# Step 2's VectorE work in two stages on two row blocks in turn: a two-layer graph kernel on one Trainium2 core

## The chip, the cores and the metric

The kernel runs on one core of one Trainium2 chip. The metric is the device time of one execution in microseconds. The engines are named as in the profile: PE (matrix products; PEld its weight loads), DVE (VectorE), ACT (ScalarE), POOL (GpSimd), SP (SyncE, which here only issues DMAs). Each engine works through its own instructions in order.

## The reference, cut to what matters

With N = 2708 nodes and 256 features, layer 0 computes `x = layernorm(x + relu([x, adj @ x] @ weight + bias))`. Layer 1 is this, followed by one more `layernorm(x + ...)`:

```
R = (adj + I) / rowsum                # sparse: about 8 entries a row
for n in range(2):
    logits = (Xa W1' W2') (Xa W3')'
    probs  = softmax(logits)
    keep   = the largest probs of a row, until their sum reaches 0.9
    A      = probs * keep / sum(probs * keep)
    Xf = R @ Xf
    Xa = A @ Xa
    Z += Xf @ U1[n]' + Xa @ U2[n]'
out = layernorm(X + Z) * g + b
```

Everything is float32. What is hard is `keep`: the smallest kept value of each row has to be found exactly, without sorting 2708 values, and equal values at the limit have to be taken in order of their place.

## The kernel before

Rows are worked on in NB = 22 blocks of P = 128 (the last, EDGE, has 20 rows). The program's stages follow each other in time: layer 0 with the dense adjacency (0 to about 285 us); step 1 of layer 1 (to 755 us), in whose begin `u1_project` makes x1 @ U1 and stores it; and step 2 (from 755 us on), the loop over `per` at L1127, which the change is about. Everything is written in the order in which each engine is to issue it; no scheduler moves anything. Waits between engines, and between instructions of one engine that depend on each other, are semaphores that the framework sets.

**Step 2, one period per row block.** In period `per` three blocks are in work. Block per+2: `logits` (PE) and `exps2` (ACT) write its exponentials, 128 x 2708, into one of four buffers es[0..3], chosen by `e2(t)`; `begin_search` (DVE) begins the search for the row's limit. Block per+1: `try_act` (ACT) evaluates two guesses of the limit with passes over the row (Relu and Sign with a summed output). Block per: DVE alone. `last_level` forms from the guesses a level that lies surely above the limit; `finish2` then

1. sets everything at or above the level to zero and sums what is below, in one pass over 2720 columns (L975, e to w),
2. takes the 8 largest of each of 20 segments of 136 columns (L978), 160 candidates,
3. sorts out the 48 largest by six rounds of MAX8 and MATCH_REPLACE8 (`put_in_order`, L575 and L577),
4. finds the limit th from their running sums (L988 to L993), and how many of the values equal to th are to be kept in each of WS = 5 parts of the row (L997 to L1003),
5. marks those in place (MATCH_REPLACE8 over 544 columns, five times, L1006), and
6. masks e in one pass (L1009) and takes the reciprocal of the kept sum (L1011).

Block per-1: PE turns the masked e (`turn`, transposes, L525), ACT copies them to wT (L528), PE multiplies with ya (`products`, L562). The period is written in NG = 6 slots g; `finish2` is a generator whose `yield`s place its parts in the slots.

**The R products.** Beside that, `r_units` (L729) issues 16 pieces of R @ Xf in each of periods 0 to 9 and 11 to 21. R is sparse: for each row block, POOL gathers 7 x 128 rows of the operand from DRAM by indirect DMA (`y_load`, L697) into one of two slots of yg, and the block's own rows come as an eighth group. The first pass (s = 0) takes x1 U1[1] from DRAM (yf_d), own rows by SP (L714); `r_out` adds to it, in place, the SBUF tile v that holds x1 U1[0] (L752), and stores the sum in v_d (L754). The second pass (s = 1, from period 11) gathers from v_d and takes its own rows from v; `r_out` calls `arrive`. When a block has both its R part and its attention part (`arrive`, L767; what came first waits in za_d and is fetched by `za_load`), `final_slot` normalizes it: statistics on DVE (L1036), scaling on ACT (L1046), two tensor operations on POOL (L1061, L1062), and the store.

**Buffers.** Tile pools hand out slots by tag in turn. "V" (22.5 KB a partition) holds layer 0's y0 and then v; "x1" holds x1 and then tile1, cut into w (DVE's work area) and scr (ACT's thrown-away output); the tag "in" has three slots for bases.

The functions that the diff touches, and their callers:

Of the kernel before, what the change touches and what calls it, by code (L numbers as in the profile page):

```python
# [9 lines left out]
FP = mybir.dt.float32  # L10
# [18 lines left out]
WS = 5  # L29
# [119 lines left out]
def fast_path(ctx, tc, c, flags, fint, xT_d, x_d, w0_d, b0_d, w1_d, w2_d, w3_d, u1_d, u2_d, g_d, b_d):  # L149
# [492 lines left out]
    v = big.tile([P, NB, D], FP, tag="V", name="v")  # L642

    def u1_project(t):
        p = rows(t)
        pz = ps_acc()
        for j in range(DC):
            nc.tensor.matmul(pz[:p], lhsT=x1T[:, j, t * P:t * P + p],  # L648
                             rhs=c.u1[:, j].rearrange("p s e -> p (s e)"), start=j == 0, stop=j == DC - 1)
        nc.scalar.copy(v[:p, t, :], pz[:p, :D])  # L650
        yf = work.tile([P, D], FP, tag="h", name="yf", bufs=5)
        nc.scalar.copy(yf[:p], pz[:p, D:])
        nc.sync.dma_start(out=c.yf_d[:p, t, :], in_=yf[:p])
# [53 lines left out]
    def r_load(s, m):  # L707
        if m not in a_in:
            a_load(m)
        if (s, m) not in y_in:  # L710
            y_load(s, m)
        y = y_in.pop((s, m))
        if s == 0:
            nc.sync.dma_start(out=y[:rows(m), CC, :], in_=c.yf_d[:rows(m), m, :])  # L714
        r_in[s, m] = a_in.pop(m), y

    def r_units(n):
        for _ in range(n):
            s, m = r_queue[0]
            p = rows(m)  # L720
            if not r_now:
                r_now[:] = [ps_misc(), 0]
                if m + 1 < NB:
                    r_load(s, m + 1)
            acc, k = r_now
            a, y = r_in[s, m]
            kw = CW if k < CC else p
            rhs = v[:p, m, :] if s and k == CC else y[:kw, k, :]
            nc.tensor.matmul(acc[:p, :D], lhsT=a[:kw, k, :p], rhs=rhs, start=k == 0, stop=k == CC)  # L729
            r_now[1] += 1  # L730
            if k == CC:
                r_now.clear()
                r_queue.pop(0)
                r_in.pop((s, m))
                base = za_load(m) if s else None
                later[1].append(lambda s=s, m=m, acc=acc, base=base: r_out(s, m, acc, base))

# [11 lines left out]
    def r_out(s, m, acc, base):  # L749
        p = rows(m)  # L750
        if s == 0:
            nc.vector.scalar_tensor_tensor(v[:p, m, :], acc[:p, :D], rinv[:p, m:m + 1], v[:p, m, :],  # L752
                                           op0=ALU.mult, op1=ALU.add)
            nc.sync.dma_start(out=c.v_d[:p, m, :], in_=v[:p, m, :])  # L754
            if m == NB - 1:
                r_load(1, 0)
        else:
            arrive(m, base, acc, rinv[:p, m:m + 1])
# [21 lines left out]

    def e2(t):
        return es[(t + 2) % 4]
# [16 lines left out]
    class Block:  # L799
# [3 lines left out]
        def __init__(self, t):  # L803
            self.t, self.p = t, rows(t)
            self.all = small.tile([P, 20], FP, tag="st2", name="st2", bufs=4)
            names = "z0 z1 z2 rz nz roots half relu sign n kept m d g l0 l1 l2 u0 u1 few".split()
            for i, n in enumerate(names):
                setattr(self, n, self.all[:self.p, i:i + 1])
            self.l, self.u = (self.l0, self.l1), (self.u0, self.u1)
            self.z = bulk[:self.p, 0, t:t + 1]  # L810
            self.nmax = small.tile([P, 1], FP, tag="nmax", name="nmax", bufs=3)[:self.p]
# [11 lines left out]
    def begin_search(b):  # L823

        nc.vector.tensor_reduce(b.z, b.all[:b.p, :NL], AX.X, ALU.add)
        nc.vector.reciprocal(b.rz, b.z)
        nc.vector.tensor_scalar(b.nz, b.z, -1.0, None, op0=ALU.mult)
        nc.vector.tensor_scalar(b.l0, b.roots, b.roots, b.rz, op0=ALU.mult, op1=ALU.mult)

# [83 lines left out]
    w = tile1[:, :NW]  # L913
    scr = tile1[:, NW:]
# [40 lines left out]
    def last_level(b):  # L955


        nc.vector.scalar_tensor_tensor(b.n, b.relu, b.rz, b.few, op0=ALU.mult, op1=ALU.is_lt)
        nc.vector.scalar_tensor_tensor(b.g, b.l1, TOP_S, b.u1, op0=ALU.mult, op1=ALU.is_gt)
        nc.vector.tensor_scalar(b.kept, b.l2, b.n, 1.0e-20, op0=ALU.mult, op1=ALU.max)  # L960
        nc.vector.scalar_tensor_tensor(b.kept, b.g, b.l1, b.kept, op0=ALU.mult, op1=ALU.max)
        level(b, b.kept)
# [3 lines left out]
    def finish2(b):  # L966

        t, p = b.t, b.p
        sc = small.tile([P, 3 + 2 * WS], FP, tag="sc", name="sc", bufs=3)
        num, run = bulk[:p, 5:, t], sc[:p, :WS]  # L970
        need, below, mass, tot = (bulk[:p, i, t:t + 1] for i in range(1, 5))
        nk = sc[:p, WS:WS + 1]
        th = b.m
        e = e2(t)[:p]
        nc.vector.scalar_tensor_tensor(w[:p], e, b.d, e, op0=ALU.is_lt, op1=ALU.mult, accum_out=below)  # L975
        cand = small.tile([P, NS2 * 8], FP, tag="cand", name="cand", bufs=2)
        for i in range(NS2):
            nc.vector.max(cand[:p, 8 * i:8 * i + 8], w[:p, SEG2 * i:SEG2 * (i + 1)])  # L978
            if i in (2, NS2 // 2 + 1):
                yield  # L980
        yield
        srt = small.tile([P, TOP1 + 1], FP, tag="srt", name="srt", bufs=3)
        s = srt[:p, :TOP2]
        put_in_order(srt, TOP2, cand, p)
        yield
# [3 lines left out]
        nc.vector.tensor_tensor_scan(x[:p, 1:TOP2 + 1], s, s, 0.0, op0=ALU.add, op1=ALU.bypass)  # L989
        nc.vector.scalar_tensor_tensor(q_, x[:p, 1:TOP2 + 1], need, s, op0=ALU.is_ge, op1=ALU.mult)  # L990
        nc.vector.tensor_reduce(th, q_, AX.X, ALU.max)
        nc.vector.scalar_tensor_tensor(q_, x[:p, :TOP2], need, s, op0=ALU.is_lt, op1=ALU.mult, accum_out=mass)
        nc.vector.tensor_scalar(q_, q_, th, None, op0=ALU.is_equal, op1=ALU.add, accum_out=nk)  # L993

        eq = small.tile([P, NS2 * 8], FP, tag="spare", name="eq", bufs=1)
        part = small.tile([P, WS, 8], FP, tag="part", name="part", bufs=1)
        nc.vector.tensor_scalar(eq[:p], cand[:p], th, None, op0=ALU.is_equal)  # L997
        nc.vector.tensor_reduce(num, eq[:p].rearrange("p (s k) -> p s k", s=WS), AX.X, ALU.add)
        nc.vector.tensor_tensor_scan(run, num, num, 0.0, op0=ALU.add, op1=ALU.bypass)
        nc.vector.scalar_tensor_tensor(run, num, nk, run, op0=ALU.add, op1=ALU.subtract)  # L1000
        nc.vector.tensor_tensor(part[:p], run[:, :, None].to_broadcast([p, WS, 8]),
                                ranks[:p, None, :].to_broadcast([p, WS, 8]), op=ALU.is_gt)
        nc.vector.tensor_scalar(part[:p], part[:p], th, None, op0=ALU.mult)  # L1003
        W = NW // WS
        for i in range(WS):
            nc.vector.match_replace(w[:p, W * i:W * (i + 1)], part[:p, i, :], e[:, W * i:W * (i + 1)], 3.0e38)  # L1006
            if i == WS // 2:
                yield
        nc.vector.scalar_tensor_tensor(e, w[:p], th, e, op0=ALU.is_gt, op1=ALU.mult, accum_out=tot)  # L1009
        ra = small.tile([P, 1], FP, tag="ra", name="ra")  # L1010
        nc.vector.reciprocal(ra[:p], tot)  # L1011
        ras[t] = ra
# [102 lines left out]
    for b in (b0, b1, b2):  # L1115
        exps2(b, 2, *logits(1, b.t, 2))
        r_units(3)
        if b is b2:
            try_dve(b0, 1)
        begin_search(b)  # L1120
        if b is b0:
            try_dve(b0, 0)
# [4 lines left out]
    for per in range(NB + 1):  # L1127
        if per == NB:
# [3 lines left out]
        b_dve = blocks.get(per)  # L1132
        t_mul = per - 1 if per else None
        if per:
            accs[t_mul] = ps_acc(t_mul)
        masks = None
        b_exp = None
        if per and per + 2 < NB:
            b_exp = blocks[per + 2] = Block(per + 2)
        for g in range(NG):  # L1140
# [11 lines left out]
            elif per:  # L1152
# [9 lines left out]
            if t_mul != EDGE:  # L1162
                products(1 if per else 0)
            if b_exp and g in (0, 1, 3):
                exps2(b_exp, (g + 1) // 2, *lg)
            if b_act:
                for k, part in {0: ((0, 0),), 1: ((0, 1), (0, 2), (0, 3)), 2: ((1, 0),), 3: ((1, 1), (1, 2), (1, 3))}.get(g, ()):
                    try_act(b_act, k, part)
            if g == 0:
                if b_dve:  # L1170
                    last_level(b_dve)
                    masks = finish2(b_dve)
                    next(masks)
                final_slot(0)
                if per > 1:

# [3 lines left out]
            elif masks:  # L1180
                next(masks, None)
                if b_exp and g == 5:
                    begin_search(b_exp)
            for f in now:
                f()
            if g and (per < NB or g < NG - 1):
# [17 lines left out]
    nc.vector.tensor_reduce(flags[:, 5 * NB:6 * NB], bulk[:, 5:, :].rearrange("p w t -> p t w"), AX.X, ALU.max)  # L1204
    nc.vector.tensor_scalar(flags[:, 5 * NB:6 * NB], flags[:, 5 * NB:6 * NB], 8.0, None, op0=ALU.is_ge)
# [389 lines left out]
```

## Time and profile before

| | us |
|---|---|
| median of 3 runs | 1348.48 (1345.78 to 1349.26) |
| the profiled execution, its own time | 1345.32 |
| its span | 1343.5 |
| first long pass of step 2 (L975) begins | 766.3 |
| last mask of step 2 (L1009) ends | 1322.6 |
| busy in the span: PE / DVE / ACT / POOL | 1246.7 / 1045.5 / 753.4 / 640.1 |
| mean granted PE clock | 0.971 |

A span runs from the first instruction to the last; the time of an execution holds some two microseconds more. A row of a timeline has the start in us from the span's begin, the duration, the engine, the line in the kernel, the operation, what it writes and reads, and in brackets the idle time before it and what ended that. The ends of PE's matmuls are modelled, and consecutive ones overlap: how fast PE goes is read from start to start.

### The profile page before, as it was taken

How to read it: one execution, taken by the hardware profiler on the slowest of the kernel's cores; microseconds unless marked ns; L12 is line 12 of the kernel's file. 1: busy time of each engine (PE TensorE's matmuls, PEld its weight loads, DVE VectorE, ACT ScalarE, POOL GpSimd, SP SyncE). 2: the span in 40 equal slices, each digit the busy share in tenths (PEclk: the TensorE clock that was granted, in tenths of full speed). 3: DMA queues.
4: the chain of work that ended last, by engine and by line, in shares of the span. 5: the costliest groups of instructions: out<-in, count | busy, mean ns of one | idle time of the engine just before them, and what ended most of it. 6: DMA issues, size and time to landing. Idle time of an engine off the chain costs nothing.

```text
span 1343.5 us, 18721 instructions
## 1 busy us (share of the span) xinstructions
PE 1246.7 (93%) x5676; PEld 881.0 (66%) x5676; DVE 1045.5 (78%) x3488; ACT 753.4 (56%) x1366; POOL 640.1 (48%) x591
## 2 busy tenths in 40 slices
PE   8999999989899999999999789999998998999885
PEld 6877878833467666667666367676765765666663
DVE  2544545865998888777751599999999999999997
ACT  1010001035556556655555567887878888999851
POOL 1000000004465522777654478877725757777770
PEclk9999999989899999999999889999998999999988
DMA  7455554512131210232223355554522633454341
GB/s 188 163 172 162 164 164 143 166 51 72 60 98 57 71 58 9 74 102 81 71 68 97 98 166 169 148 160 147 161 66 92 191 119 122 150 172 146 122 144 37
DMA packets 92829, 157.92 MB, mean 118 GB/s; under 512 B 16356, under 2 KB 65196, under 8 KB 92720
## 3 DMA queue, kind: packets, MB, share of 16 engines
q1 hardware_dynamic: 66434, 100.59, 23.6%
q0 software_dynamic: 20544, 51.17, 13.4%
q10 hardware_dynamic: 5742, 4.89, 1.3%
q8 instruction: 47, 0.77, 0.2%
q14 instruction: 62, 0.51, 0.1%
HBM read 125.33 MB, written 31.26 MB: 117 GB/s over the span
## 4 chain that ended last, share of the span: by engine, by line
PE 54%; DVE 38%; ACT 4%; issue 2%; POOL 1%; DMA 1%; SPq 0%; ACTq 0%; DVEq 0%; POOLq 0%
PE acc L562 16%; PE acc L255 15%; PE lg L505 6%; DVE cand L978 6%; DVE w L1006 5%; DVE e L1009 5%; DVE w L975 4%; PE tr L525 4%; DVE srt L575 3%; DVE spare L577 3%; PE misc L676 3%; PE acc L648 2%; PE acc L460 2%; PE misc L424 2%; PE misc L390 2%
## 5 line engine op out<-in xcount | busy, mean ns | idle before, releaser
L528 ACT COPY wT<-tr 128x512 f32<-128x512 f32 (+2 forms) x258 | 131.9, 519 | 223.4 <-PE tr L525 219.0
L562 PE MATMUL acc<-ya,wT 128*128 128x256 f32 (+1 forms) x924 | 236.3, 396 | 12.1 <-ACT wT L528 11.7
L697 POOL DMA_INDIRECT yg<-yf_d,ix x154 | 194.8, 1265 | 78.7 <-PE misc L729 40.6
L697 POOL DMA_INDIRECT yg<-v_d,ix x154 | 193.8, 1259 | 79.4 <-DMA v_d<-v 34.0
L562 PE MATMUL acc<-x,wT 128*128 128x256 f32 (+1 forms) x924 | 230.5, 388 | 0.0
L562 PEld LDWEIGHTS acc<-x,wT 128*128 128x128 f32 (+1 forms) x924 | 165.2, 189 | 79.6 <-issue 46.9
L562 PEld LDWEIGHTS acc<-ya,wT 128*128 128x128 f32 (+1 forms) x924 | 172.1, 194 | 68.2 <-ACT wT L528 23.1
L255 PE MATMUL acc<-y,adj_t 128*128 128x257 f32 (+1 forms) x924 | 208.4, 381 | 0.0
L255 PEld LDWEIGHTS acc<-y,adj_t 128*128 128x128 f32 (+1 forms) x924 | 171.8, 189 | 32.7 <-issue 8.9
L365 POOL DMA_INDIRECT adj_t<-in_adj,ix x154 | 164.7, 1069 | 51.5 <-issue 39.9
L729 PE MATMUL misc<-yg,adj_t 128*128 128x256 f32 (+1 forms) x660 | 173.9, 397 | 9.4 <-DVE v L752 9.4
L505 PE MATMUL lg<-k,q 64*128 64x512 f32 (+3 forms) x528 | 150.7, 598 | 21.5 <-ACT e L821 19.5
L525 PE MATMUL tr<-ident,e 128*128 128x128 f32 (+2 forms) x946 | 149.9, 278 | 18.0 <-DVE e L1009 17.9
L729 PEld LDWEIGHTS misc<-yg,adj_t 128*128 128x128 f32 (+1 forms) x660 | 118.4, 193 | 56.1 <-issue 16.2
L525 PEld LDWEIGHTS tr<-ident,e 128*128 128x128 f32 (+2 forms) x946 | 114.0, 141 | 62.2 <-issue 23.9
L332 POOL DMA_DIRECT2D part_d<-e x1 | 0.6, 576 | 286.9 <-DVE e L331 286.9
L568 DVE MAX8 cand<-e 128x8 f32<-128x170 f32 (+1 forms) x352 | 87.3, 318 | 35.4 <-ACT e L512 35.4
L921 ACT ACTIVATE w<-e,st 128x2708 f32<-128x2708 f32 (+1 forms) x43 | 113.5, 2640 | 0.0
L437 ACT COPY x1T<-tr 128x256 f32<-128x256 f32 (+1 forms) x22 | 8.0, 364 | 186.6 <-PE tr L436 186.6
L924 ACT ACTIVATE w<-e,st 128x2708 f32<-128x2708 f32 (+1 forms) x42 | 110.9, 2641 | 0.1
L978 DVE MAX8 cand<-w 128x8 f32<-128x136 f32 (+1 forms) x440 | 93.5, 284 | 0.8
L575 DVE MAX8 srt<-spare 128x8 f32<-128x128 f32 (+3 forms) x264 | 81.3, 308 | 9.1
(228 smaller groups left out, 1761.8 us busy)
## 6 DMA issues: line engine op xcount, KB each, us to landing
adj_t<-in_adj SPq DMA_DIRECT2D x44, 704.0 KB
adj_t<-adjc_d SPq DMA_DIRECT2D x44, 448.0 KB
adjc_d<-adj_t SPq DMA_DIRECT2D x22, 256.0 KB
base<-za_d SPq DMA_DIRECT2D x41, 128.0 KB
adjc_d<-adj_t SPq DMA_DIRECT2D x22, 192.0 KB
xt<-in_x ACTq DMA_DIRECT2D x21, 128.0 KB
x_d<-x SPq DMA_DIRECT2D x21, 128.0 KB
x1b_d<-xb SPq DMA_DIRECT2D x21, 128.0 KB
```

What stands on the lines that cost most here:

```text
L255: nc.tensor.matmul(acc[:p, :n], lhsT=halves[k // KH][:kw, k % KH, :p], rhs=y[:kw, k, :n], start=k == 0, stop=stop and k == NB - 1)
L365: nc.gpsimd.indirect_dma_start(out=a[:CW, i, :], out_offset=None, in_=adj_rows, in_offset=bass.IndirectOffsetOnAxis(ap=ix[:CW, m, i:i + 1] ...
L505: nc.tensor.matmul(lg[:p, h, :b - a], lhsT=q[o, t * P:t * P + p], rhs=keys[s][o, i, :b - a], start=True, stop=True)
L525: nc.tensor.transpose(tr[:kw, k % 4, :p], e[:p, k * P:k * P + kw], ident[:p, :p])
L528: nc.scalar.copy(wT[:, :full, :p], tr[:, :full, :p])
L562: nc.tensor.matmul(acc[:p, :D], lhsT=wT[:kw, k % 4, :p], rhs=y[:kw, k, :], start=k == 0, stop=k == NB - 1)
L575: nc.vector.max(dst[:p, i:i + 8], src[:p])
L697: nc.gpsimd.indirect_dma_start(out=y[:CW, i, :], out_offset=None, in_=rows_d, in_offset=bass.IndirectOffsetOnAxis(ap=ix[:CW, m, i:i + 1], ...
L729: nc.tensor.matmul(acc[:p, :D], lhsT=a[:kw, k, :p], rhs=rhs, start=k == 0, stop=k == CC)
L921: nc.scalar.activation(scr[:b.p, :N], e, AF.Relu, bias=b.nz, scale=b.l[k], accum_out=b.relu)
L924: nc.scalar.activation(scr[:b.p, :N], e, AF.Sign, bias=b.nz, scale=b.l[k], accum_out=b.sign)
L978: nc.vector.max(cand[:p, 8 * i:8 * i + 8], w[:p, SEG2 * i:SEG2 * (i + 1)])
```

## The change

Step 2's DVE work on a block is cut in two stages, and a period now does stage one of block `per` and stage two of block `per-1`, an instruction of one after an instruction of the other wherever both have some:

- Stage one: `last_level`, `below_level` (the pass of 1.) and `candidates` (2.). Stage two: `in_order` (3.), `threshold` (4.), `mark` (5.) and `mask` (6.). `vector_slots` hands them to the six slots by `turns`; `begin_search` of block per+2 is set between the marks and ahead of the mask.
- Block per-2 is turned and multiplied in period `per`, one period later than before. The loop has 24 periods instead of 23.
- The below-level pass writes to an area of its own, `low`; `w` is left to the marks and the mask. Exponentials have five buffers instead of four: `e4` and `scr` take the room of v (tile2, tag "V").
- v is no longer kept in SBUF. `u1_project` copies both halves of its product with one ACT instruction into a ring of 11 slots, and stores both (yf_d and v_d) by SP. `r_out` of the first pass gets its base by `v_load` from v_d; the own rows of the second pass come from v_d by SP too.
- Equal values are counted in WS = 4 parts of 680 columns instead of 5 of 544, with a scan that begins at the number to be kept; one small instruction (L1000) goes.

The long passes are the same two per block. The lines of the diff that the steps speak of:

```
-    v = big.tile([P, NB, D], FP, tag="V", name="v")
+    VS = NB // 2
+    v_out = big.tile([P, VS, 2, D], FP, tag="V", name="v_out")
...
-        nc.scalar.copy(v[:p, t, :], pz[:p, :D])
-        yf = work.tile([P, D], FP, tag="h", name="yf", bufs=5)
-        nc.scalar.copy(yf[:p], pz[:p, D:])
-        nc.sync.dma_start(out=c.yf_d[:p, t, :], in_=yf[:p])
+        o = v_out[:p, t % VS]
+        nc.scalar.copy(o.rearrange("p s d -> p (s d)"), pz[:p])
+        nc.sync.dma_start(out=c.yf_d[:p, t, :], in_=o[:, 1, :])
+        nc.sync.dma_start(out=c.v_d[:p, t, :], in_=o[:, 0, :])
...
-        if s == 0:
-            nc.sync.dma_start(out=y[:rows(m), CC, :], in_=c.yf_d[:rows(m), m, :])
+        nc.sync.dma_start(out=y[:rows(m), CC, :], in_=(c.yf_d, c.v_d)[s][:rows(m), m, :])
...
-                base = za_load(m) if s else None
+                base = za_load(m) if s else v_load(m)
...
-            nc.vector.scalar_tensor_tensor(v[:p, m, :], acc[:p, :D], rinv[:p, m:m + 1], v[:p, m, :],
+            nc.vector.scalar_tensor_tensor(base[:p], acc[:p, :D], rinv[:p, m:m + 1], base[:p],
                                            op0=ALU.mult, op1=ALU.add)
-            nc.sync.dma_start(out=c.v_d[:p, m, :], in_=v[:p, m, :])
+            nc.sync.dma_start(out=c.v_d[:p, m, :], in_=base[:p])
...
+    def vector_slots(a, b, begin):
+        order = in_order(b) if b else None
+        levels = last_level(a) if a else None
+        cands = candidates(a) if a else None
+        limits = threshold(b) if b else None
+        run_all(turns((part_of_it(order, 7) if b else None, 1), (levels, 1)))
+        yield
+        if a:
+            below_level(a)
+        yield
+        run_all(turns((order, 1), (part_of_it(cands, 8) if a else None, 2)))
+        if a and not b:
+            run_all(part_of_it(cands, 8))
+        yield
+        run_all(turns((limits, 1), (cands, 2)))
+        yield
+        if b:
+            mark(b, 0)
+            mark(b, 1)
+        yield
+        for i in (2, 3):
+            if b:
+                mark(b, i)
+            if begin:
+                next(begin)
+        if begin:
+            run_all(begin)
+        if b:
+            mask(b)
+        yield
...
-    for per in range(NB + 1):
+    for per in range(NB + 2):
...
-        t_mul = per - 1 if per else None
+        t_mul = per - 2 if per > 1 else None
...
+        vector = vector_slots(blocks.get(per), blocks.get(per - 1), begin_search(b_exp) if b_exp else None)
...
+            next(vector)
             if g == 0:
-                if b_dve:
-                    last_level(b_dve)
-                    masks = finish2(b_dve)
-                    next(masks)
                 final_slot(0)
```

`turns` takes from each stream in turn the given number of steps until all are done. `in_order`, `candidates`, `last_level` and `threshold` are the old instructions with a `yield` after each (or after a few); `below_level`, `mark` and `mask` are single instructions of the old `finish2`, the last with its reciprocal.

## The prediction

> **What bounds the kernel now.** I read the windows by stage first (columns: stretch, length, then busy us and instructions of PE, weight loads, DVE, ACT, POOL, then granted clock, DMA share, GB/s), then single instructions. Step 2 runs from 766 to 1323 us: 22 row blocks, one a period, each period opened by the long pass of L975.
>
> ```profile
> 900.00:1000.00 100.00, 94.97 (x453) 69.07 (x451) 95.75 (x328) 81.96 (x138) 63.70 (x48) 1.00 0.44 131
> 1100.00:1200.00 100.00, 89.66 (x400) 63.46 (x400) 95.90 (x328) 91.15 (x150) 77.42 (x65) 0.97 0.45 138
> ```
>
> DVE is busy 95.8 of 100 us, and the view of waits shows no DVE wait of 150 ns or more between 766 and 1330 us. It is the bound, and what is left are short gaps. The timeline shows where (start, duration, instruction):
>
> ```profile
> 910.26 0.17 DVE L1011 RECIPROCAL ra<-bulk 128x1 f32<-128x1 f32 x1
> 910.34 0.14 DVE L825 TENSOR_REDUCE bulk<-st 128x1 f32<-128x3 f32 x1
> ...
> 911.59 0.22 DVE L961 SCALAR_TENSOR_TENSOR st<-st 128x1 f32<-128x1 f32 x1
> 911.84 0.16 DVE L941 RECIPROCAL st<-st 128x1 f32<-128x1 f32 x1
> 912.04 0.21 DVE L942 TENSOR_SCALAR st<-st,bulk 128x1 f32<-128x1 f32 x1
> 912.29 3.05 DVE L975 SCALAR_TENSOR_TENSOR w<-e,st 128x2720 f32<-128x2720 f32 x1
> ...
> 936.73 3.05 DVE L975 SCALAR_TENSOR_TENSOR w<-e,st 128x2720 f32<-128x2720 f32 x1
> ```
>
> L825 uses nothing of L1011 and starts 0.09 before its end. L941 uses L961's result and starts 0.03 after its end. So following one's own producer costs about 0.08 + 0.036 = 0.115 us. The last two lines give the period: 936.73 - 912.29 = 24.44 us. From period 12 on, when finished rows are also normalized, it is 26.8 (1164.63 to 1191.71 is one).
>
> The same stretch for PE, and a late one for POOL:
>
> ```profile
> 914.26 1.13 PE L505 MATMUL lg<-k,q 64*128 64x512 f32 x4 [0.32 <-ACT e L821]
> ...
> 934.80 0.63 PE L525 MATMUL tr<-ident,e 128*128 128x128 f32 x4 [0.94 <-DVE e L1009]
> ```
>
> ```profile
> 1163.68 0.95 POOL L697 DMA_INDIRECT yg<-v_d,ix  x1 [0.30 <-PE tr L525]
> 1164.93 3.56 POOL L697 DMA_INDIRECT yg<-v_d,ix  x1 [0.30 <-issue]
> 1168.80 0.95 POOL L697 DMA_INDIRECT yg<-v_d,ix  x1 [0.30 <-issue]
> 1170.05 0.95 POOL L697 DMA_INDIRECT yg<-v_d,ix  x1 [0.30 <-issue]
> 1172.12 0.73 POOL L1061 TENSOR_TENSOR yg<-yg,gb 128x256 f32<-128x256 f32 x1 [1.12 <-ACT yg L1046]
> ```
>
> PE sat idle 0.32 + 0.94 = 1.26 us in that period: it needs some 23.2 of the 24.44. POOL issues a gather every 1.25 us, 14 a period = 17.5. A gather that meets a long VectorE pass takes 3.56 instead of 0.95 (the pass of 1164.63 ends at 1167.68), so the two long passes of a period cost POOL 2 x 2.6 = 5.2. Together 22.7; late periods add four tensor operations (some 3.3 with their gaps): 26.0. Two resources stand close behind the first.
>
> **What the Trainium skill says.** VectorE: DVE Perf Modes, section "The DRAIN you can't avoid", says that after every operation the next waits until the pipeline is empty, and that chained operations cost the same with and without semaphores. The trace differs: -0.08 us without a wait, +0.036 with one. The measurement decides; if the page were right, rival C below would hold. SBUF — State Buffer, section "Who interferes with whom", says that an operation with two SBUF inputs takes only the read side of the port pair shared with GpSimd, and infers that descriptor generation is not stalled by it. The trace shows 3.56 against 0.95 us beside L975, which has two such inputs: I count the stall.
>
> **The change, part by part.**
>
> *Interleaving (vector_slots).* Before, 29 instructions of a period wait for the DVE instruction just ahead: 11 in the sort (L575/L577), 4 around the level up to L975, 11 from L990 to L1009, and three singly (L826, the first L978, L1011). After, sort steps of block t-1 alternate with level steps of block t, then with candidates, and the threshold with candidates. In the new order four still follow their producer: the second pass over q_, the product that makes part, the first mark, and the reciprocal after the mask. One goes with L1000: 24 x 0.115 = 2.76 us. I replayed both orders with the durations of the rows and the two gaps (-0.083, +0.037): 24.48 before (measured 24.44), 21.2 after, with what follows included.
>
> *Four parts instead of five.* Five replaces of 128x544 at 0.709 + 0.07 become four of 128x680: 0.709 + 136/0.96 GHz = 0.85, + 0.07. Net -0.2 us. One small operation (L1000, 0.225) goes: -0.26 with its gap. The replay holds both.
>
> *The bound that takes over.* DVE at 21.2 lies below PE (23.2 less part of the 0.32, as nmax now follows the mask at once: I take 23.1) and POOL (22.7). ACT, at 82 of 100 us early, needs 20.0. So early periods take 23.1, not 21.2. Period 10 has no R product, hence no gathers and less PE work: about 21.0. Late periods: DVE 26.85 - 3.25 = 23.6, ACT 0.91 x 26.8 = 24.4, POOL 26.0 if both stalls hit and it never waits; one stall partly falls into its idle time, so 25.7.
>
> *The added stage.* Period 0 holds only stage one of block 0. DVE then needs block 1's search from ACT, whose last instruction before was at 778.2: 12.0 us instead of 24. At the end a period is added for stage two of block 21 alone: the same sort and threshold, not interleaved, marks and mask 13.3 by the replay, and arrivals and statistics: 17.0.
>
> *v in DRAM.* 22 stores in u1_project, 22 loads for r_out and 22 own-row loads in the second pass, 128 KB each, on SP's queue at some 0.45 us: about 12 issues = 5.4 us of a period. 8.6 MB beside 158. In a period, the load of the even block's v stands behind the store of the odd block and is used after the sort, threshold and two marks, over 9 us later. A za_d load took 4.77 us in the chain of waits. Cost nothing on that cover; without it, up to 2.5 us for each of 22 r_outs, below nothing excluded, as the old v was in SBUF. The own-row load waits for PE's slot, as the yf load before it did. POOL's queue gets one memset before step 2, behind ACT copies long done: nothing.
>
> *u1_project.* Two ACT copies of 0.37 become one (0.57, nearest row the 128x512 copy), but between 290 and 318 us the chain is PE's own matmuls. Only at its two ends does ACT stand in it: -0.5 (0 to -3). Stores for yf wait on no scarcer buffer: the gathers that read them start at 711.
>
> *Sum.* Before, first long pass to end of the last mask: 1322.6 - 766.3 = 556.3. After: periods 0 and 1 12.0 + 21.7; eight of 23.1 = 184.8; period 10 21.0; 11 and 12 (before 24.3 and 25.7) 23.2 + 24.4; eight of 25.7 = 205.6; period 21 (no more gathers) 23.5; the added one 17.0: 533.2. Difference -23.1, with u1 -23.6. The tail of 20.9 after the last mask stays. Against the profiled execution's 1345.3: 1321.7. That execution lies 3.2 under the median of the runs; I allow for less than half of it: **1323**, of its own 1309 to 1333.
>
> **Rivals.** (A) *POOL keeps its pace*, stalls falling as now and waits staying between: 24.0 early, 26.6 late. Same sum: 33.7 + 192 + 21 + 49.5 + 212.8 + 23.5 + 17 = 549.5, so -7.3: 1338. For it: of an early period all but 24.4 - 22.7 = 1.7 us is taken. Against it: POOL waited for PE's slots then. (B) *PE and POOL yield*, all runs at DVE's pace, 21.2 and 23.6: about 496, so -60: 1285. Against it: PE's own matmuls, start to start, are 44 products and 32 of R at 0.216, 22 transposes 2.7 and 12 logits 3.2: 22.3 us. (C) *No gap is saved* (the page's DRAIN, or the waits still bind): periods fall by the 0.4 of the parts only, the added stage eats it: 1345, no change. Against it: the replay. (D) *Slower: r_out waits for v's load* in DVE's in-order queue, with candidates, mask and so PE's transposes behind it. DVE has 23.1 - 21.2 = 1.9 us of slack in each of ten early periods, 19 in all; the gain is 23.6, so it turns above (19 + 23.6)/22 = 1.9 us a load. At 2.4 us: 52.8 - 42.6 = +10: 1355. For it: 4.77 us landing, SP in order. Against it: the 9 us.
>
> **Chances.** Forecast 0.60, A 0.20, B 0.07, C 0.05, D 0.08. Range 1303 to 1340: the forecast's own with A, and below it some of B's direction; B, C and D, 2 in 10, are left out. Faster 0.87, same 0.05, slower 0.08, with 0.3% (4 us) as what a measurement of this kernel tells from no change.
>
> **What would show it.** In the changed profile: long passes (L994) 23.1 us apart early and 25 to 26 late; DVE waits now longer than 150 ns, ended by PE or ACT, where there were none; POOL with hardly a wait late; the step from a sort instruction to the next dependent one hidden. Wrong if L994 stays 24.4 apart (A, C by whether DVE waits), if it comes to 21.2 (B), or if r_out (L756) sits behind base<-v_d (D).

## The result, and the profile after

The changed kernel takes 1335.36 us (median of 4 runs, 1334.9 to 1337.52); the kernel before took 1348.7 beside it. The ratio is 0.9909, with a 95% interval from 0.9891 to 0.9926: faster by some 13 us, where 25.5 were forecast. The profiled span is 1333.5 us.

The chain that ended last in the page before, then the lines of busy time and of that chain in the page after:

```profile
PE 54%; DVE 38%; ACT 4%; issue 2%; POOL 1%; DMA 1%; SPq 0%; ACTq 0%; DVEq 0%; POOLq 0%
...
PE 1245.0 (93%) x5676; PEld 880.6 (66%) x5676; DVE 1001.6 (75%) x3420; ACT 754.5 (57%) x1348; POOL 639.1 (48%) x594
...
PE 71%; ACT 14%; DVE 11%; issue 3%; DMA 1%; POOL 0%; ACTq 0%; DVEq 0%
```

DVE's busy time fell from 1045.5 to 1001.6 us, and its share of the chain is 11% where it was 38%. So DVE's work did get shorter, and over most of step 2 DVE does not bound any more. The windows after that answer to the two of before (stretch, length, then busy us and instructions of PE, weight loads, DVE, ACT, POOL, then granted clock, DMA share, GB/s):

```profile
900.00:1000.00 100.00, 97.12 (x463) 70.01 (x463) 91.25 (x328) 83.56 (x140) 61.80 (x49) 1.00 0.48 136
1100.00:1200.00 100.00, 91.43 (x420) 66.21 (x420) 90.41 (x325) 92.91 (x153) 78.77 (x69) 0.98 0.54 163
```

PE is at 97 early, ACT at 93 late, DVE at 91 and 90. What the turns did to the sort is seen in DVE's timeline (start, duration):

```profile
906.49 0.31 DVE L1013 MATCH_REPLACE8 spare<-srt,spare 128x160 f32<-128x160 f32 x1
906.71 0.49 DVE L1001 MAX8 cand<-w 128x8 f32<-128x136 f32 x2
907.12 0.31 DVE L1010 MAX8 srt<-spare 128x8 f32<-128x160 f32 x1
907.35 0.48 DVE L1001 MAX8 cand<-w 128x8 f32<-128x136 f32 x2
907.75 0.07 DVE L1013 MATCH_VALUE_LOAD spare<-srt,spare 128x8 f32 x1
```

Between a sort step and the next that needs it stand two candidates' MAX8 of the other block, and each instruction starts 0.07 to 0.09 us before its forerunner's end. Counted from the starts and ends of an early period's instructions, gaps under 150 ns go from 29 (1.01 us) before to 4 (0.14 us) after, as forecast. But DVE now waits, mostly in one place. Its waits from 766 to 1330 us (us in total, times, longest):

```profile
DVE bulk L831 <- ACT e L823: 41.0, 19, 4.6
DVE base L756 <- PE misc L728: 5.3, 3, 2.3
DVE st L974 <- ACT st L953: 2.3, 1, 2.3
```

L831 is the sum in `begin_search` that needs all exponentials of the row. Before, the same view showed no DVE wait in this stretch.

The kernel by stages, from the end of one mask (L1059) to the next, in the span's time and read to about 0.1 us. Periods 0 and 1 run from the first long pass (L994, 767.2) to the first mask:

| term of the sum | forecast | measured |
|---|---|---|
| start of step 2, against before | -0.5 | +0.9 |
| periods 0 and 1 | 12.0 + 21.7 = 33.7 | 41.6 |
| eight early periods, 2 to 9 | 8 x 23.1 = 184.8 | 184.2 |
| period 10 | 21.0 | 23.0 |
| periods 11 and 12 | 23.2 + 24.4 = 47.6 | 48.3 |
| eight late periods, 13 to 20 | 8 x 25.7 = 205.6 | 209.0 |
| period 21 | 23.5 | 23.5 |
| the added period | 17.0 | 15.7 |
| after the last mask | 20.9 | 21.0 |

From the first pass to the last mask that is 545.3 us against 533.2: 12.1 too many. With 1.4 of the start and 0.1 of the tail it makes the 13.6 by which the span of 1333.5 misses the forecast one (1343.5 - 23.6 = 1319.9). More than half of it is in periods 0 and 1. The 1.4 of the start says little: in a second run of the changed kernel step 2 starts at 766.2. The late periods hide more than their 3.4: the first is 25.7 and the last (20) 23.5, but the six between are 26.6 to 26.7, hardly less than before (26.8). Of the early ones period 2 is 21.1 (22.6 in the second run) and the others 23.3. In periods 20 and 21, which have no exponentials left to make, DVE is full again: 23.1 of work and 0.4 of short gaps make their 23.5.

Windows, same columns. First the kernel before, from its first long pass to its first mask; then the kernel after: periods 0 and 1, an early period, period 10, a late one:

```profile
766.30:788.80 22.50, 10.72 (x37) 8.14 (x37) 21.59 (x68) 11.81 (x17) 17.93 (x16) 0.81 0.56 167
...
767.20:808.80 41.60, 27.64 (x78) 17.10 (x79) 29.29 (x100) 29.19 (x43) 33.07 (x29) 0.79 0.61 181
876.40:899.80 23.40, 23.09 (x112) 17.16 (x110) 21.24 (x78) 20.02 (x35) 18.83 (x16) 1.00 0.58 175
993.00:1016.00 23.00, 18.81 (x81) 12.04 (x80) 20.50 (x76) 19.88 (x34) 11.52 (x11) 0.93 0.41 127
1143.30:1170.00 26.70, 23.86 (x111) 16.97 (x110) 24.28 (x88) 24.91 (x42) 21.10 (x19) 1.00 0.53 158
```

The early one shows an engine that is nearly full (PE). In periods 0 and 1 it is POOL: 33.07 us and 0.30 of gap at each of 29 instructions make 41.8 of 41.6. That alone proves nothing, since POOL was full in the same sense in the window of before (17.93 and 16 gaps make 22.7 of 22.5), where DVE had no wait. PE's granted clock was 0.79 in this window, and about the same, 0.81, in that of before. In period 10 and the late one no engine is full. What holds them is an order and not an amount of work.

**The first two periods.** The chain of waits from 767 to 808.8 us is by line, in its first terms:

```profile
by line: PE misc L728 26.0%; DMA yg<-yf_d,ix 26.0%; issue 11.6%; PE lg L505 8.4%; ACT e L937 6.5%; ACT e L940 6.3%; POOL yg L698 6.0%; ACT e L823 4.8%; DVE base L756 1.0%; ACT st L945 0.9%; ACT st L943 0.7%; ACT st L951 0.7%; DVE st L984 0.
```

R products (L728) and the gathers they wait for are over half of it (26.0 and 26.0%). POOL's timeline in the middle of the stretch:

```profile
789.67 0.95 POOL L698 DMA_INDIRECT yg<-yf_d,ix  x1 [0.30 <-issue]
790.92 0.95 POOL L698 DMA_INDIRECT yg<-yf_d,ix  x1 [0.30 <-issue]
792.17 0.95 POOL L698 DMA_INDIRECT yg<-yf_d,ix  x1 [0.30 <-issue]
```

A gather every 1.25 us, without a pause from 771 to 809 us. Logits stand behind the R products in PE's order, and ACT waits for the logits (L505) for 11.3 us at a stretch.

**ACT's copy.** ACT's timeline of the early period, with the idle time and what ended it in brackets:

```profile
876.51 0.25 ACT L531 COPY wT<-tr 20x128 f32<-20x128 f32 x1
879.91 0.59 ACT L528 COPY wT<-tr 128x512 f32<-128x512 f32 x1 [3.15 <-PE tr L525]
880.39 1.12 ACT L823 ACTIVATE e<-lg,nmax 128x1024 f32<-128x1024 f32 x1
```

The same in the late period, with the load of the square root's table and that of the exponential's after it:

```profile
1143.64 1.28 ACT L1172 ACT_TABLE_LOAD   x1
1144.93 0.30 ACT L1172 ACTIVATE sds<-mvs,eps 128x4 f32<-128x4 f32 x1
1146.75 0.59 ACT L528 COPY wT<-tr 128x512 f32<-128x512 f32 x1 [1.52 <-PE tr L525]
1147.34 1.28 ACT L823 ACT_TABLE_LOAD   x1
1148.64 1.11 ACT L823 ACTIVATE e<-lg,nmax 128x1024 f32<-128x1024 f32 x1
```

Each period begins on ACT with the copy of the transposes just asked of PE. PE first does its R products and the last products of the block before. The row's first exponentials (L823), whose logits were made at the end of the period before, stand behind that copy. The late period is 24.9 of ACT's work, some 0.3 of its short gaps and 1.52 of this wait: 26.7.

These are the theories that the experiments test. *Mine*: R products and their gathers hold periods 0 and 1; ACT's order holds period 10 and the late ones; PE holds the early ones. *Rivals*: POOL is full late (the prediction's own term); DVE's starts still set the pace; v's way through DRAM costs something.

### The profile page after: what moved, and what is told of

It is laid out like the page before. It is cut to its first block, busy times and chain, and to the rows that moved or that the text cites. A ratio compares the mean times of both kernels' runs of the same rounds, so it can differ in the third digit from the quotient of the medians.

```text
span 1333.5 us, 18733 instructions
## 1 busy us (share of the span) xinstructions
PE 1245.0 (93%) x5676; PEld 880.6 (66%) x5676; DVE 1001.6 (75%) x3420; ACT 754.5 (57%) x1348; POOL 639.1 (48%) x594
## 4 chain that ended last, share of the span: by engine, by line
PE 71%; ACT 14%; DVE 11%; issue 3%; DMA 1%; POOL 0%; ACTq 0%; DVEq 0%
PE acc L562 24%; PE acc L255 15%; PE lg L505 8%; PE tr L525 6%; PE misc L728 5%; PE misc L677 3%; ACT e L937 3%; ACT e L823 3%; PE acc L649 2%; DVE e L1059 2%; ACT e L940 2%; PE acc L460 2%; PE misc L424 2%; PE misc L390 2%; ACT wT L528 2%
## 5 line engine op out<-in xcount | busy, mean ns | idle before, releaser
L698 POOL DMA_INDIRECT yg<-v_d,ix x154 | 194.9, 1265 | 73.7 <-PE lg L505 27.1
L562 PEld LDWEIGHTS acc<-ya,wT 128*128 128x128 f32 (+1 forms) x924 | 170.9, 194 | 66.6 <-ACT wT L528 22.9
L728 PE MATMUL misc<-yg,adj_t 128*128 128x256 f32 (+1 forms) x704 | 185.1, 398 | 12.6 <-DMA yg<-yf_d,ix 6.9
L505 PE MATMUL lg<-k,q 64*128 64x512 f32 (+3 forms) x528 | 152.1, 604 | 26.8 <-ACT e L827 22.4
L728 PEld LDWEIGHTS misc<-yg,adj_t 128*128 128x128 f32 (+1 forms) x704 | 126.5, 193 | 64.8 <-issue 17.0
L937 ACT ACTIVATE e<-e,st 128x2708 f32<-128x2708 f32 (+1 forms) x43 | 113.5, 2640 | 0.1
L940 ACT ACTIVATE e<-e,st 128x2708 f32<-128x2708 f32 (+1 forms) x42 | 110.9, 2642 | 0.1
L1001 DVE MAX8 cand<-w 128x8 f32<-128x136 f32 (+1 forms) x440 | 106.9, 285 | 0.0
L505 PEld LDWEIGHTS lg<-k,q 64*128 64x128 f32 (+1 forms) x528 | 39.3, 183 | 61.7 <-ACT e L827 30.1
```

The source lines that it names most:

```text
L505: nc.tensor.matmul(lg[:p, h, :b - a], lhsT=q[o, t * P:t * P + p], rhs=keys[s][o, i, :b - a], start=True, stop=True)
L562: nc.tensor.matmul(acc[:p, :D], lhsT=wT[:kw, k % 4, :p], rhs=y[:kw, k, :], start=k == 0, stop=k == NB - 1)
L698: nc.gpsimd.indirect_dma_start(out=y[:CW, i, :], out_offset=None, in_=rows_d, in_offset=bass.IndirectOffsetOnAxis(ap=ix[:CW, m, i:i + 1], ...
L728: nc.tensor.matmul(acc[:p, :D], lhsT=a[:kw, k, :p], rhs=y[:kw, k, :], start=k == 0, stop=k == CC)
L937: nc.scalar.activation(scr[:b.p, :N], e, AF.Relu, bias=b.nz, scale=b.l[k], accum_out=b.relu)
L940: nc.scalar.activation(scr[:b.p, :N], e, AF.Sign, bias=b.nz, scale=b.l[k], accum_out=b.sign)
```

## The experiments

The runs of v alone, four parts alone, the first one without turns and the one with the search last were on a chip where all kernels took some 2% longer (the kernel before 1378.17 us); they are read by their ratios to the kernel before on that chip.

### v in DRAM alone

The kernel before, with v stored and loaded as in the change:

```
+        nc.sync.dma_start(out=c.v_d[:p, t, :], in_=o[:, 0, :])
...
-                base = za_load(m) if s else None
+                base = za_load(m) if s else v_load(m)
```

> The kernel before with v kept in DRAM alone (one ACT copy and two stores in u1_project, v_load for r_out, own rows from v_d), all else as before. If the 66 added transfers are covered, as the prediction has it: no change, 1346 to 1350 us, no DVE wait at r_out's line. Rival D (r_out waits for v's load): 22 waits of up to 2.5 us on the engine that bounds this kernel, so up to +55 us, and at least +7 if only a tenth of that shows.

Measured: 1.0003 (0.9985 to 1.002). v in DRAM costs nothing that can be measured (the interval is some 2.4 us to either side), as forecast, and rival D falls.

### Four parts alone

The kernel before with one line changed:

```
-WS = 5
+WS = 4
```

> The kernel before with four parts for equal values instead of five, alone. DVE bounds step 2 here, so each saved DVE time should count in full: one replace's fixed part and one load of its values, about 0.2 us a block, 22 blocks: -4.4 us, 1344. If DVE were not the bound of the kernel before: 0.

Measured: 0.9966 (0.9948 to 0.9984), 0.34% or some 4.6 us, with an interval from 2 to 7. This is in the kernel before, where DVE bounds; what the four parts are worth in the changed kernel was not measured. In which periods it lies isn't settled, since the early ones scatter between 24.1 and 25.0 us on that chip.

### Without turns

The changed kernel, the two streams of DVE work one after the other in each part:

```
-        streams = [(f, n) for f, n in streams if f is not None]
-        while streams:
...
+        for f, n in streams:
+            if f is not None:
+                yield from f
```

> The changed kernel with the streams of a slot one after the other instead of in turn; two stages, buffers and parts stay. If the alternation is what shortened DVE's period: DVE needs 21.2 + 24 x 0.115 = 24.0 us early and 26.4 late, so early periods go from 23.3 to 24.0, late ones stay near 26.7: +6 to +10 us, about 1343. If the two stages alone did it (PE's or ACT's order): no change, 1335.

Measured: 0.9951 (0.9936 to 0.9965), with early periods of 23.3 and late ones of 26.6 to 26.7. That is what the changed kernel showed with turns on the first chip. So neither expectation holds: the early periods aren't 24.0, and the total isn't that of the changed kernel (0.9909). It was run once more beside the changed kernel itself, on a chip like the first:

> The changed kernel itself, to stand beside the next two on one chip. All theories: ratio to the kernel before 0.991, about 1335 us where the kernel before takes 1348; eight early periods of 23.3 us, late ones of 26.6 to 26.7.

> The changed kernel with its two streams of VectorE work one after the other inside each part instead of instruction by instruction. On the earlier chip it showed the same steady lengths as the changed kernel shows here (23.3 early, 26.6 to 26.7 late), but was not beside it. Theory (in the steady periods TensorE and ACT set the pace, so turns buy nothing there; they buy only where DVE's own pace shows: periods 0 and 1 and the last two): 23.3 and 26.7 again, periods 20 and 21 some 2 us longer each (25.5 and 25.0 instead of 23.5 and 23.4), total 1339 to 1344, 4 to 8 us over the changed kernel. Rival (DVE's pace still sets the early periods; prediction's arithmetic): early 24.0, total 1343 to 1348. Rival (turns are worth nothing anywhere): 1335.

Measured: the changed kernel 1335.22, ratio 0.9919 (0.9903 to 0.9935); without turns 1340.38, ratio 0.9953 (0.9937 to 0.9969). Windows of an early and a late period without turns:

```profile
899.50:922.90 23.40, 23.08 (x112) 17.14 (x110) 22.50 (x78) 20.04 (x35) 18.57 (x16) 1.00 0.58 175
1143.80:1170.30 26.50, 23.58 (x111) 16.79 (x110) 25.70 (x86) 24.73 (x40) 21.01 (x19) 1.00 0.51 159
```

The lengths are the same as with turns, to 0.4 us. DVE is busy 22.5 instead of 21.2 early and waits only 0.2; with its 20 short gaps (0.70 us) that fills the period. Late, 25.7 of work and 0.8 of gaps fill it too. So without turns DVE is full, and it is by chance that its pace then equals what PE and ACT allow. The turns themselves are worth 5.2 us. These lie where DVE's pace shows: periods 20 and 21 (25.5 + 25.0 against 23.5 + 23.4: 3.6), period 12 (0.9) and the tail (23.2 against 21.2; not followed up); the rest of the profiled difference (6.0) cancels. The first rival's 24.0 early is refuted. The split in two stages alone already puts other instructions between dependent ones, and hid 9 of the 29 gaps.

### ACT's first exponentials ahead of its copy

The changed kernel, with ACT's order at the start of a period turned round:

```
                 r_units(n)
+                if b_exp:
+                    exps2(b_exp, 0, *lg)
...
-            if b_exp and g in (0, 1, 3):
+            if b_exp and g in (1, 3):
```

> The changed kernel with ACT's first exponentials of a period (exps2, part 0) put ahead of its first copy of the transposes, so that ACT has work while PE gets there. Theory ACT (ACT's own work of 20.2 us early and 25.1 late, plus 1.5 to 3 us in which it waits for the period's first transposes, is one round of a loop and sets period 10 and the late periods): period 10 from 23.0 to about 20.5, late ones from 26.6 to about 25.3, early ones from 23.3 to 22.9: -12 to -18 us. Theory POOL (gathers and finals set the late periods): period 10 shorter, late ones stay at 26.6: -3 to -5 us.

Measured: 1314.46 (1311.31 to 1314.48), ratio 0.9742 (0.9725 to 0.9758): some 21 us under the changed kernel (12 to 18 were expected), for the place of one ACT block in its queue. Its windows (early, period 10, late):

```profile
895.30:918.20 22.90, 22.90 (x112) 17.22 (x110) 21.23 (x77) 20.12 (x35) 18.64 (x15) 1.00 0.55 173
987.00:1009.20 22.20, 18.84 (x88) 11.87 (x88) 20.68 (x77) 20.09 (x35) 10.38 (x9) 1.00 0.37 119
1129.10:1154.20 25.10, 23.78 (x111) 16.97 (x110) 23.75 (x88) 24.81 (x42) 20.81 (x19) 1.00 0.56 168
```

Now PE is full early (22.90 of 22.90), and ACT late (24.81 of 25.10, with no wait of 150 ns or more). Late periods are 1.6 us shorter, about the wait that went (1.52). Period 10 fell to 22.2 only, where 20.5 was expected; in it ACT still has 1.9 us of waits. ACT's wait for the first transposes is half as long early, because it has work in the meantime:

```profile
897.70 1.11 ACT L827 ACTIVATE e<-lg,st 128x1024 f32<-128x1024 f32 x1
898.71 0.19 ACT L827 ACTIVATION_READ_ACCUMULATOR e<-lg,st 128x1 f32 x1
900.46 0.59 ACT L528 COPY wT<-tr 128x512 f32<-128x512 f32 x1 [1.56 <-PE tr L525]
```

### No root, no table loads

The last norms take Identity in place of the square root; this kernel leaves the root out, and with it both table loads of a late period.

```
-mvs[:, a:b, 1], AF.Sqrt, bias=c.eps, scale=1.0)
+mvs[:, a:b, 1], AF.Identity, bias=c.eps, scale=1.0)
```

> The changed kernel with Identity in place of the square root of the last normalizations, which leaves out the root and with it two table loads of 1.28 us on ACT in each late period; nothing else moves. Theory ACT: late periods from 26.6 to POOL's own 25.3 or so, -9 to -12 us. Theory POOL: late periods stay at 26.6, 0 to -3 us.

Measured: 1325.14 in a single run, 10 us less than the changed kernel. Early periods stay 23.3; late ones go from 26.65 to 25.25. Its late window, then ACT's wait in it:

```profile
1138.80:1164.00 25.20, 23.77 (x110) 16.97 (x110) 23.66 (x86) 22.04 (x39) 20.91 (x19) 1.00 0.56 167
```

```profile
ACT wT L528 <- PE tr L525: 2.9, 1, 2.9
```

ACT's work is 2.9 us less, but its wait for the transposes grows from 1.5 to 2.9: half of the work taken from ACT comes back as waiting. PE has 23.77 us of work in this window, and 1.4 us of waits for ACT make up its 25.2.

### POOL's two operations moved to DVE

The changed kernel, with the product and the sum of the last norm on DVE in slot 3:

```
-            nc.gpsimd.tensor_tensor(h[:p], h[:p], c.gb[:p, 0, :], op=ALU.mult)
-            nc.gpsimd.tensor_tensor(h[:p], h[:p], self.x1[:p], op=ALU.add)
...
+                nc.vector.tensor_tensor(h[:p], h[:p], c.gb[:p, 0, :], op=ALU.mult)
+                nc.vector.tensor_tensor(h[:p], h[:p], x1[:p], op=ALU.add)
```

> The changed kernel with the two tensor operations of each normalized block (3.1 us a late period on POOL) on DVE in slot 3 instead, 1.7 us more for DVE, which waits 2 us a period now. Theory POOL: late periods from 26.6 to about 25, -10 to -15 us. Theory ACT: late periods stay at 26.6 within 0.3, 0 to -3 us.

Measured: 1336.53 in a single run, no change. Its late window:

```profile
1143.00:1169.60 26.60, 23.78 (x110) 16.96 (x110) 24.80 (x90) 24.80 (x41) 19.12 (x16) 1.00 0.53 164
```

POOL has 2 us less to do (19.12 for 21.10), and the period is as long as in the changed kernel. POOL is not what holds the late periods.

### Fewer R products first

The changed kernel with 8 R products in period 0, 16 in period 1, and 17 in each of periods 2 to 9, where all of these had 16:

```
+    units = {0: 8, 1: 16}
+    units.update({p: (each - first - 24) * (p - 1) // 8 - (each - first - 24) * (p - 2) // 8 for p in range(2, 10)})
```

> The changed kernel with 8 pieces of R in period 0 and 16 in period 1 was 16 and 16: here 8 and 16, the other 8 spread over periods 2 to 9 (17 each). If the first two periods took 41.6 instead of 33.7 us because PE stood in the R products waiting for gathers, with logits and so ACT behind it: the mask of block 0 ends about 5 us earlier, each of eight periods costs up to 0.4 more: -2 to -5 us. If they are held by something else: 0 to +3.

Measured: 1327.32 (1326.02 to 1329.87), ratio 0.9851 (0.9835 to 0.9868), 8 us under the changed kernel, more than the 2 to 5 that were expected. The window of periods 0 and 1:

```profile
765.10:797.40 32.30, 20.04 (x64) 11.75 (x64) 28.30 (x99) 29.10 (x43) 25.90 (x22) 0.89 0.58 173
```

32.3 us in place of 41.6, with PE's waits for gathers down from 6.9 to 3.1. After ACT's search for block 1 is done (777.3), DVE is busy 20.0 of the 20.1 us to the first mask: here it is DVE that bounds. The run takes out 7 gathers and some 14 matmuls together, so it shows that the R work held these periods, and not how much of that was gathers and how much products. Of these 9.3 periods 2 to 10 give back 3.2 (periods 3 to 9 are now 23.7 to 23.8), and period 11 wins 1.7 (23.3 for 25.0).

### Both

The two edits together. The counts of 19 or 20 and of 18 products in the expectation are wrong: it is 17 in periods 2 to 9, and 16 in the changed kernel. Only 8 products are put off, not 24, so it is luck in part that the total came out as expected.

> The changed kernel with two edits at once: ACT's first exponentials of a row ahead of turn 0's copy (alone 1314.46 us) and 8, 16 and then 19 or 20 R products a period instead of 18 each (alone 1327.32 us against 1335.36). Theory (the two edits meet different bounds, but share one budget, TensorE's): the first two periods lose some 10 us of waiting for gathers; the 24 products put off cost about 0.235 us each on TensorE, which now has no gaps in the early periods (22.9 of 22.9 us busy), so that eight early periods go from 22.9 to about 23.25 us and periods 1 and 2, which were short (20.6, 21.2), to 23.2 as well. Sum about 1308 us, between 1305 and 1312; late periods 25.0 us as with the first edit alone. Rival (independent savings add): 1304 us or less, early periods still 22.9. Rival (the first periods' loss was ACT's order too, already gone): 1314, no gain over the first edit alone.

Measured: 1310.49 (1307.14 to 1311.49), ratio 0.9734 (0.9717 to 0.975). This is the lowest median of all, though its interval overlaps that of the first edit alone (0.9742), measured on another chip with a median 4 us higher. Periods 0 and 1 are 32.2 us, where they are 41.3 with the first edit alone, and periods 4 to 9 are 23.3 to 24.7 in place of 22.6 to 23.0. The savings don't add. Against the first edit alone the first mask ends 9.9 us earlier (798.1, 808.0) and the last 5.0 earlier (1286.8, 1291.8). PE, full in the early periods, takes most of the other 4.9 back: the 8 products put off are 16 matmuls of 0.216 us (start to start, as in the kernel before), an estimate of 3.5 us. The remaining 1.4 stay open. An early window:

```profile
888.10:911.40 23.30, 23.30 (x114) 17.55 (x114) 20.93 (x77) 20.15 (x34) 18.73 (x16) 1.00 0.60 176
```

### The first exponentials first, without turns

The edit that puts ACT's first exponentials ahead and the one that takes the turns out, together.

> The kernel with ACT's first exponentials put first (22.9 early, 25.0 late, 1314.46 us), with the two streams of VectorE work one after the other instead of in turn. Theory (once ACT no longer waits, DVE's dependent starts show again): in the late periods DVE has 25.8 us of work without turns against ACT's 25.0, so 25.9 late, and early 23.2 (22.4 busy and its starts) instead of 22.9; with the last two periods about 1325 to 1331, 11 to 16 us over the kernel with turns. Rival (turns buy nothing in the steady periods even then): 22.9 and 25.0 again, 1318 to 1321.

Measured: 1327.91 (1323.43 to 1328.08), ratio 0.9855 (0.9835 to 0.9875), against 0.9742 with turns, on another chip: 1.1%, some 15 us by the ratios and 13.5 by the medians and the profiled spans. Its windows (early, late):

```profile
899.40:922.50 23.10, 23.10 (x112) 17.40 (x111) 22.40 (x78) 19.98 (x33) 18.53 (x16) 1.00 0.59 177
1137.10:1162.50 25.40, 23.92 (x110) 16.90 (x110) 24.54 (x89) 24.88 (x41) 17.98 (x19) 1.00 0.54 166
```

The total is as expected, but not where it was expected. An early period loses 0.1 and a late one 0.3 (25.3 in place of 25.0; 25.9 had been expected). The rest is in periods 2 (22.6 for 20.6), 3 (23.0 for 21.2), 12 and 13 (2.7 together), 20 and 21 (2.2 together) and the tail (23.0 for 20.8). DVE is full in the late ones, but with 24.5 us of work and 0.8 of gaps, not with the 25.8 expected from the other kernel without turns. There three small operations of the threshold (L1035, L1046, L1049) ran beside POOL's TENSOR_TENSORs and took 0.77, 0.62 and 0.76 us; here POOL is done with these before, and they take 0.27, 0.19 and 0.26. Turns are worth 5 us in the kernel as changed and 13 to 15 in the one with ACT's order mended.

### The next search after the mask

The changed kernel with `begin_search` of block per+2 after the mask, not between the marks and ahead of it:

```
         for i in (2, 3):
             if b:
                 mark(b, i)
-            if begin:
-                next(begin)
-        if begin:
-            run_all(begin)
         if b:
             mask(b)
+        if begin:
+            run_all(begin)
```

> The changed kernel with begin_search after the mask instead of between the marks and ahead of it. In the changed kernel the first step of begin_search waits about 2 us a period for ACT's exponentials, with the last mark and the mask behind it. If that held mask holds PE's transposes (rival): periods 1 to 2 us shorter, -20 to -40 us. If PE (early) and ACT's or POOL's round (late) set the period: no change within 3 us.

Measured: 0.9989 (0.9972 to 1.0006), worse than the kernel without turns on the same chip (0.9951). Neither expectation had it slower. Late periods are up to 28.1 to 28.2 there against 26.7. In a late one ACT waits twice as long for the transposes as in the changed kernel:

```profile
ACT wT L528 <- PE tr L525: 3.0, 1, 3.0
```

With its 24.7 of work in a window of 28.0 that is again ACT's round. So the search's place ahead of the mask is no loss of the change; why the wait grew by 1.5 us was not followed.

## Why the prediction was half right

The direction held; the size, 13 us where 25.5 were forecast, did not. The step that failed is the sum by stages: it took for the length of a stage the work of one engine, and put at nothing the waits that the order of the queues forces. In periods 0 and 1 that is the wait behind R products and their gathers, 7.9 us in all; in period 10 and the late ones it is ACT's wait for the first transposes, with 2.0 us in the one and a net 3.4 in the eight others. That 1335 lies within 1303 to 1340 is no merit of the mechanism: the range was drawn to take in rival A. A's sum for step 2 (549.5 us) is nearer to the measured 545.3 than the forecast's 533.2, and A's cause, POOL, is refuted.

- **"The interleaving saves 2.76 us a period on DVE": right as work, wrong as time.** The gaps went as counted (29 to 4), and with them DVE from 24.44 us a period to 21.2 of work and 2 of waiting. The Trainium skill, VectorE: DVE Perf Modes, section "The DRAIN you can't avoid", says that the next operation waits until the pipeline is empty and that semaphores between chained operations cost nothing extra; taken so, no order would shorten anything. It also says that a next operation that isn't held starts earlier, which the prediction left out. The gaps of the trace (-0.08 without a wait and +0.036 us with one) held for the changed order too, and they decide. But the stage split without turns gives the same steady periods, so turns bring 5.2 us of the 13.
- **"Early periods take 23.1, PE's": right.** Measured 23.3, with PE busy for 23.0 of it, and with ACT's order mended PE full at 22.9. That the eight come to 184.2, under the forecast 184.8, is luck: it hangs on the short period 2.
- **"The added stage: 12.0 us instead of 24" for period 0, and 21.7 for period 1: the largest miss, 7.9 us.** The 12.0 held: ACT's last instruction for block 1's search (L953) ends 12.1 us after the first pass. From there to the first mask it took 29.4 us, not 21.7. I asked only what DVE waits for. Period 0 still issued the 16 R products of a full period, whose 14 gathers take POOL 17.5 us by the prediction's own figure, and 12.0 us have no room for them. PE waited at these products, the logits stood behind them, and ACT waited for the logits. With 8 and 16 products the same two stretches take 12.1 and 20.1 us, and DVE is full in the second: the DVE figure was sound, the R work around it was put at nothing.
- **"ACT 0.91 x 26.8 = 24.4" and "POOL 26.0, so 25.7" late: wrong engine, and 1 us too short.** POOL was not it (no change with 2 us less work). The figure for ACT was near: its work is 24.9 us, of which the loads of tables are 2.56. What was left out is its wait for PE's first transposes, which adds 1.5. A busy share of before says what an engine did in that period, not how long its own loop is: that contains waits that its order puts there, and they don't go when another engine is relieved. At 26.65 the late loop gives hardly anything against DVE's old 26.8. (The pair of starts that the prediction names for 26.8, 1164.63 and 1191.71, is 27.1 apart; most late periods before were 26.8.) The same wait (2.9 us) makes period 10 23.0 where DVE's 21.0 was forecast; there the mended order took 0.8 off.
- **Period 21, 23.5: right**, and 23.6 was the prediction's own figure for DVE late, which is full there. **The added period, 17.0: 15.7**, 1.3 us too much.
- **"Four parts, -0.2": right in the kernel before.** Alone 4.6 us in all (2 to 7), against 0.2 x 22 = 4.4.
- **"v in DRAM: nothing": right.** Ratio 1.0003; no wait of r_out for v's load in the trace after.
- **The rivals.** A's late length (26.6) came true, but by ACT and not by POOL; its early 24.0 did not. B is refuted by early periods of 23.3, C by the gaps, and D by v alone.

## What to carry to other kernels

In this kernel, when the engine that bound was relieved, the next bound wasn't the next one by busy time but the next loop of waits. So write down each engine's queue for one period, with what every instruction waits for, and add work and forced waits. Then try to put ahead whatever in an in-order queue is ready; here one block of ACT's exponentials moved ahead of a copy brought 21 us, more than the whole change. And a pipeline stage that is added can leave a short first period: take the side work (here R products and their gathers) out of it, as a period's share no longer fits.

## What the runs showed of the hardware

- A switch of ACT's table takes 1.28 us, and the instruction behind it starts 0.01 to 0.02 after its end (1143.64, 1.28, then 1144.93). The Trainium skill, ScalarE activation tables: per-element evaluation and per-set limits, section "What a function is on this engine", says 1283 ns, and the trace agrees. Another page of the Trainium skill, ScalarE: Activation LUTs, section "What ACT_TABLE_LOAD costs", adds some 1.38 us of drain to it, 2.66 in all; no such pause stands before or after the load in this trace.
- The gather that meets a long DVE pass is held up in the changed kernel too: 3.42 and 3.35 us in a late period, in place of 0.95. Of 41 gathers from 755 us on that took over 1.5 us, 39 overlap one of the long passes (L994, L1059, and those of the same form just before), and every one of these ends 0.81 to 0.83 us after the pass does. With them POOL is kept busy, and yet it was not the bound.
- The other way it looks alike: in the second run without turns three small DVE operations (L1035, L1046, L1049) took 0.62 to 0.77 us beside POOL's TENSOR_TENSORs (1182 to 1185 us), and each ended 0.04 to 0.06 us after one of these. Apart from them they take 0.19 to 0.27 us. No run isolates this.
